# Layer 0's mixture of experts: the output bias row and the running counts of the experts as matrix products, and a shorter gating sum

## The chip, the cores and the metric

The kernel runs on one core of one Trainium2 chip. The metric is the time of one launch on the device, in microseconds (us). Lower is better. A profile of one further execution shows every engine: TensorE (PE, with its weight loads PEld apart), VectorE (DVE), ScalarE (ACT), GpSimd (POOL) and SyncE (SP).

## The reference, cut to what matters

The whole program is a decoder of two layers, each with self-attention, cross-attention and a feed-forward part, over 32 sequences of 100 tokens with 256 features, all in float32. The change lies in the third of these six parts, the feed-forward part of layer 0. That part is itself a small transformer block with a mixture of experts:

```
q, k, v  = in_proj(rope(layernorm(x))) per head     # 16 heads of 16; q, k, v have biases
x1       = layernorm(x + attention(q,k,v) @ out_proj_w.T + out_proj_b)
logits   = x1 @ gate_w.T + gate_b                   # 8 experts
gates    = softmax(logits); keep the two largest, gates unchanged by the others' removal
moe      = sum over the two kept experts of gate * (x1 @ expert_w[e].T + expert_b[e])
result   = layernorm(x1 + moe)
```

The softmax goes over all eight experts, and the two largest of its values weigh the two experts' outputs. Each row of x1 is processed by only two experts, so the kernel writes every row twice into a list that is sorted by expert, and multiplies whole tiles of 128 rows by one expert's weights.

## The kernel before

**The stage.** The 32 sequences lie in 8 groups `g` of 4 (`G = 4`, `T = 100` tokens each). `heads_attention` (line 286) runs the attention as a software pipeline over steps `s` = 0 to 32, one sequence each. Its order of instructions is written out by hand and kept as written on TensorE, VectorE, ScalarE, GpSimd and the DMA queue. A step does, for the sequence `s + 1`, `scores` (32 x 100 products, line 363), `masked` (VectorE adds the causal mask, line 372), `lowered` (VectorE finds the maximum, line 383; GpSimd subtracts it, line 384) and `exponentials` (ScalarE, line 389); for the sequence `s`, `turn_weights` (TensorE turns the weights in four tiles, line 396; ScalarE copies each, tile `eT`, line 401) and `sums` (line 412); for the sequence `s - 1`, `divided` (TensorE turns, line 425; VectorE takes reciprocals `rc` and divides, tile `o`, lines 430 and 432), `turn_sums` (lines 438 and 444) and `output` (`project`, line 230: two matrix products of `oT` with `f0_wo`, then `res`, line 1396, in which VectorE adds the PSUM tile to the residual rows `xl`). TensorE writes `mm` tiles in PSUM, of which there are four; a product can't start before the tile that it takes is read by its last reader.

**What is filled in.** Between these parts `fill(s, part)` puts other work, by the table `plan`, in which the entry `(i, part)` under the key `away` holds for the group `w + away` with `s = 4 w + i`:

- the norm, rotation and projection of groups that come next (`ahead_norm`, `queries`);
- `output_bias(g)` (line 1401), once for each group, before its first `res` (for group 0 in step 0, for group 1 in step 1, for each later group in the first step of the group before it): VectorE adds the row `out_row` (the output projection's bias and the values' bias times the projection, made once by `output_row`) to the group's 100 x 1024 residual values;
- `rows_of` (the statistics and the norm of finished rows, giving x1) and `gating`, in parts: 0 to 2 turn x1 and form the logits; 5 adds the gate bias, finds the maximum and subtracts it (lines 1450 to 1452); 5.5 takes the exponential (line 1454); 6 sums, inverts, multiplies (lines 1458, 1459 and 1461, tile `gt`) and finds the two largest (`top2`, lines 1109 and 1110); 6.5 makes the one-hot masks `hot`, copies the gates (line 1469) and, on GpSimd, forms `hs` and `hc`, the counts of each expert by row and by sequence; 7 sums these by three products with the triangle and the ones of `before0` (lines 1481, 1485 and 1489); 8 adds the counts of earlier groups `base` (lines 1498 and 1502), picks the place of each row by the one-hot masks (lines 1504 and 1505) and casts it to an integer `pos0` (line 1506);
- `send0`: GpSimd writes the rows of one sequence to their places by two indirect DMAs (line 1517), in steps 12 to 32 in every step, after its last `lowered` of the step;
- `table`, in the last steps: VectorE makes the list of tiles.

**After the attention** the loop over tiles of 128 rows runs (`turned0`, `product`): TensorE turns a tile, multiplies it by one expert's weights, and the result goes back to DRAM. The gating of the last two groups runs between these tiles.

**What sets the order.** All queues are in order. The instruction that waits holds back all that stands behind it on its engine.

Of the kernel before, what the change touches and what calls it, by code (L numbers as in the profile page):

```python
# [10 lines left out]
F32 = mybir.dt.float32  # L11
# [7 lines left out]
P = 128  # L19
B, T, D = 32, 100, 256  # L20
S2, DC = 361, 192
G = 4
# [44 lines left out]
def kernel(ctx: ExitStack, tc: tile.TileContext, io: dict, out: bass.AP):  # L67
# [215 lines left out]
        load_x(g)  # L283


    def heads_attention(pool, w, wo, bias, norm, turn, res, fill, ready=0, order=()):

# [160 lines left out]
        def output(s):  # L448
            oT = oTs.pop(s)
            ps = mm_tile()  # L450
            project(ps[:T, :D], [oT[:, k, :] for k in range(2)], [wo[:, k, :] for k in range(2)])
            res(s, ps[:T, :D])

        fill.queries, fill.turned = queries_or_keys, turned_
# [81 lines left out]
    def list_of(g):  # L536

        return int(g >= SPLIT[1])
# [776 lines left out]
    with tc.tile_pool(name="f0x", bufs=1) as fixed, tc.tile_pool(name="f0", bufs=2) as pool:  # L1315
# [31 lines left out]
                shift[:, c, :], less[:, c : c + 1].to_broadcast([P, P]), 1.0 / D, None, ALU.mult  # L1347
            )

        out_row = fixed.tile([T, D], F32, name="out_row")  # L1350
        nc.sync.dma_start(out_row, io["f0_bo"].to_broadcast([T, D]))

        def output_row():
            own = fixed.tile([P, 2, T], F32, name="own_values")
            for c in range(2):
                nc.vector.tensor_scalar(
                    own[:, c, :], col("f0_bv", c).to_broadcast([P, T]), 1.0, None, ALU.mult
                )
            ps = mm_tile()
            project(  # L1360
                ps[:T, :D], [own[:, c, :] for c in range(2)], [f0_wo[:, c, :] for c in range(2)]
            )
            nc.vector.tensor_tensor(out_row, ps[:T, :D], out_row, ALU.add)

        biases, heldx = {}, {}

# [29 lines left out]
            nc.vector.tensor_tensor(xi, xi, ps, ALU.add)  # L1396

        x1s, x1Ts, parts = {}, {}, {}

        def output_bias(g):  # L1400
            nc.vector.tensor_tensor(xls[g], xls[g], bc(out_row, 1, G), ALU.add)

        def rows_of(g, part):

# [15 lines left out]
        def gating(g, part):  # L1420
            if part == 0:
                heldx[g] = [mm_tile() for _ in range(2)]
                for c in range(2):
                    for i in range(G):
                        nc.tensor.transpose(
                            heldx[g][c][:, i * T : (i + 1) * T],
                            x1s[g][:, i, c * P : (c + 1) * P], ident[:T, :T],
                        )
            elif part == 1:
                x1T = x1Ts[g] = pool.tile([P, 2, GT], F32, tag="x1T", name="x1T", bufs=1)  # L1430
                for c in range(2):
                    nc.scalar.activation(
                        x1T[:, c, :], heldx[g][c][:, :GT], AF.Identity,
                        bias=col("f0_ln1b", c), scale=col("f0_ln1w", c),
                    )
            elif part == 2:
                x1T = x1Ts.pop(g)
                pg = heldx[g] = mm_tile()
                for i in range(G):
                    project(  # L1440
                        pg[:T, i * E : (i + 1) * E],
                        [x1T[:, c, i * T : (i + 1) * T] for c in range(2)],
                        [f0_wg[:, c, :] for c in range(2)],
                    )
            elif part == 5:
                pg = heldx.pop(g)
                lg = parts[g] = small.tile([T, G, E], F32, tag="lg", name="lg")
                p3 = pg[:T, : G * E].rearrange("p (g e) -> p g e", e=E)
                nmx = small.tile([T, G], F32, tag="nmg", name="nmg")
                nc.vector.tensor_tensor(lg, p3, bc(row("f0_gb"), 1, G), ALU.add)  # L1450
                nc.vector.tensor_reduce(nmx, lg, AX.X, ALU.max, negate=True)
                nc.vector.tensor_tensor(lg, lg, bc(nmx, 2, E), ALU.add)
            elif part == 5.5:
                nc.scalar.activation(parts[g], parts[g], AF.Exp)
            elif part == 6:
                lg = parts.pop(g)
                sm = small.tile([T, G], F32, tag="smg", name="smg")
                nc.vector.tensor_reduce(sm, lg, AX.X, ALU.add)
                nc.vector.reciprocal(sm, sm)
                gt = small.tile([T, G, E], F32, tag="gt", name="gt")  # L1460
                nc.vector.tensor_tensor(gt, lg, bc(sm, 2, E), ALU.mult)
                parts[g] = top2(pool, gt, G)
            elif part == 6.5:
                own = slice(g * G, (g + 1) * G)
                top, hot = top2(
                    pool, None, G, row("iota", P), which0[:, :, own].rearrange("t k g -> t g k"),
                    parts[g],
                )
                nc.gpsimd.tensor_copy(gates0[:, own, :], top[:T, :, 0:2])
                hs = pool.tile([T, G, E], F32, tag="hs", name="hs")  # L1470
                hc = pool.tile([T, G + 1, E], F32, tag="hc", name="hc")
                nc.gpsimd.tensor_tensor(hs, hot[:T, 0], hot[:T, 1], ALU.add)
                nc.gpsimd.memset(hc[:, 0], 0.0)
                for i in range(G):
                    nc.gpsimd.tensor_tensor(hc[:, i + 1], hc[:, i], hs[:, i], ALU.add)
                parts[g] = hot, hs, hc
            elif part == 7:
                hot, hs, hc = parts[g]
                pl = heldx[g] = mm_tile()
                n = G * E  # L1480
# [4 lines left out]
                nc.tensor.matmul(  # L1485
                    pl[:, :n], before0[:, 1, :], hc[:, :G].rearrange("p i e -> p (i e)"),
                    start=False, stop=True,
                )
                nc.tensor.matmul(
                    pl[:, n : n + E], before0[:, 1, :], hc[:, G], start=True, stop=True  # L1490
                )
            else:
                hot, hs, hc = parts.pop(g)
                pl = heldx.pop(g)
                n = G * E
                base = base0[list_of(g)]
                at = pool.tile([T, G, E], F32, tag="at", name="at")
                nc.vector.tensor_tensor(
                    at, pl[:T, :n].rearrange("p (i e) -> p i e", e=E), bc(base[:T], 1, G),
                    ALU.add,  # L1500
                )
                nc.vector.tensor_tensor(base, base, pl[:, n : n + E], ALU.add)
                own = slice(g * G, (g + 1) * G)
# [151 lines left out]
        def ahead_norm(g, part):  # L1655
# [10 lines left out]
                (3, 3): ((ahead_norm, 3.1),),  # L1666
            },
            1: {
                (0, 2): ((ahead_norm, 3.2), (output_bias,)), (1, 1): ((queries, 0),),
                (1, 2): ((queries, 1),), (2, 1): ((queries, 2),), (2, 2): ((queries, 3),),  # L1670
            },
            0: {(3, 2): ((rows_of, 0),)},
# [15 lines left out]
        def fill(s, part):  # L1688

            w, i = s // G, s % G  # L1690
            if s == 0 and part == 0:
                output_row()
            for away, events in plan.items():
                g = w + away
                if 0 <= g < NG and (away < 1 or g >= 2):
                    for f, *args in events.get((i, part), ()):
                        if s < B or f is not gating:
                            f(g, *(args if s < B or f is not send0 else (1,)))
            if s < 2 and part == 2:
                output_bias(s)  # L1700
            if s == B and part == 0:
                send0(SPLIT[1], 0)
            if (s, part) in CONSTANTS:
                make_constants(CONSTANTS[s, part])
            if s < 2 * E and s % 2 == 0 and part in (1, 2):
                expert_weights(s // 2, part - 1)
                if part == 2 and s // 2 + 2 < E:
                    expert_bias(s // 2 + 2)
            first = G * (SPLIT[1] + 2)
            if part == 2 and 0 <= s - first < 5:  # L1710
                table(0, s - first)
            if (s, part) in ((B - 1, 3), (B, 1)):
                for n in range(AHEAD // 2):
                    fetch((s - B + 1) * (AHEAD // 2) + n)
# [1194 lines left out]
```

## Time and profile before

| what | us |
|---|---|
| median of 3 runs | 3312.29 |
| lowest and highest run | 3305.76 and 3319.2 |
| the profiled execution's own time | 3304.47 |
| its span, first to last instruction | 3302.7 |
| `scores` of the 2nd step to `scores` of the last one, in the profile | 758.13 to 1024.06 |

The span is cut into lines of code: a row of the profile names the line, the engine, the operation, the tile that is written and the tiles that are read, the shape, the number of instructions, their busy time and the mean of one, and then the idle time of the engine just before them, with what ended it. A row "A <- B" among the waits says that A's engine stood idle until B was done. The granted clock is TensorE's, 1.00 at full speed; its mean over the span is 0.982.

### The profile page before, as it was taken

The numbers are of one execution on the slowest core, as the hardware profiler recorded it, in microseconds if no ns is written. First come the engines' busy times: TensorE is split into PE (matmuls) and PEld (weight loads), VectorE is DVE, ScalarE is ACT, GpSimd is POOL, SyncE is SP. The second block draws the span as 40 slices with busy tenths as digits, with TensorE's granted clock in tenths as the row PEclk, the third lists the DMA queues.
The fourth block names the chain that finished last, engine by engine and source line by source line (L and its number), as shares of the span: only waits on it lengthen the run. The fifth ranks groups of instructions, "written<-read, shape, count | busy, mean of one in ns | idle before, by whom it ended". The sixth has DMA issues, their size and how long they took to land. (4 is left out here: it accounts for less than half of the span.)

```text
span 3302.7 us, 66245 instructions
## 1 busy us (share of the span) xinstructions
PE 3155.7 (96%) x25158; PEld 2155.8 (65%) x25158; DVE 1823.4 (55%) x5227; ACT 1660.2 (50%) x3701; POOL 1335.6 (40%) x1191
## 2 busy tenths in 40 slices
PE   8998999989998899998999999999999999999998
PEld 6775666656776543334666666666666667899998
DVE  6777666758886578875446555564656451011111
ACT  5665666666664366674555554454555442211111
POOL 3445888866775532201223333333333332012222
PEclk9999999999998999998999999999999999999999
DMA  9401211101012722001000100000000003456665
GB/s 301 158 15 55 56 51 51 48 21 40 25 35 74 220 70 53 26 1 46 10 15 22 34 15 25 17 28 24 16 26 21 25 13 107 134 183 189 179 181 159
DMA packets 165700, 228.71 MB, mean 69 GB/s; under 512 B 22846, under 2 KB 139618, under 8 KB 164998
## 3 DMA queue, kind: packets, MB, share of 16 engines
q1 hardware_dynamic: 133592, 185.22, 18.0%
q0 software_dynamic: 20304, 27.99, 4.0%
q10 hardware_dynamic: 11486, 11.23, 1.0%
q8 instruction: 204, 3.34, 0.4%
q14 instruction: 114, 0.93, 0.1%
HBM read 150.92 MB, written 73.41 MB: 68 GB/s over the span
## 5 line engine op out<-in xcount | busy, mean ns | idle before, releaser
L2289 POOL TENSOR_TENSOR ex<-ex,rc 100x1444 f32<-100x1444 f32 x128 | 331.6, 2591 | 769.5 <-DVE rc L2288 532.0
L2280 ACT ACTIVATE ex<-s,nmx 100x361 f32<-100x361 f32 x512 | 303.2, 594 | 121.6 <-DVE nmx L2271 121.6
L384 POOL TENSOR_TENSOR s<-s,nmx 100x800 f32<-100x800 f32 x128 | 199.6, 1561 | 206.2 <-DVE nmx L383 110.9
L1852 ACT ACTIVATE h<-sc,cols 128x800 f32<-128x800 f32 x256 | 222.0, 924 | 93.1 <-PE sc L1846 91.4
L2740 POOL DMA_INDIRECT out_x<-y,xg x53 | 83.0, 1565 | 425.3 <-DVE y L2739 243.8
L2271 DVE CUSTOM_DVE_ANT_0 s<-sc,mb 100x361 f32<-100x361 f32 x512 | 250.7, 528 | 7.5 <-PE sc L2264 7.5
L2722 ACT ACTIVATE hgT<-sc 128x1024 f32<-128x1024 f32 x53 | 54.3, 1024 | 326.1 <-PE sc L230 326.1
L2739 DVE TENSOR_SCALAR y<-mm,gx 128x256 f32<-128x256 f32 x53 | 25.7, 484 | 323.2 <-PE mm L230 323.2
L230 PE MATMUL sc<-xgT,w1b 128*128 128x128 f32 x1696 | 198.1, 275 | 0.5 <-DMA w1b<-in_f_w 0.5
L2264 PE MATMUL sc<-kT,qT 64*100 64x361 f32 x1024 | 197.6, 463 | 0.0
L230 PEld LDWEIGHTS sc<-xgT,w1b 128*128 128x128 f32 x1696 | 193.6, 192 | 0.8 <-DVE xgT L2707 0.7
L230 PE MATMUL mm<-wx,hgT 128*128 x848 | 191.6, 379 | 0.0
L2236 PE MATMUL mm<-x_wa,cT 128*128 128x512 f32 (+1 forms) x512 | 188.8, 491 | 0.2
L2314 PEld LDWEIGHTS mm<-eT,vb 128*64 128x64 f32 (+1 forms) x3072 | 136.8, 137 | 67.3 <-issue 66.4
L2206 PE MATMUL mm<-cT,x_wa 128*128 128x361 f32 x512 | 179.7, 470 | 1.0 <-ACT lnT L142 0.9
L2296 PE MATMUL mm<-ident,ex 100*128 100x100 f32 (+1 forms) x1536 | 166.6, 257 | 10.1 <-ACT kT L2218 5.5
L2303 ACT COPY eT<-mm 128x400 f32<-128x400 f32 (+1 forms) x256 | 125.6, 491 | 100.1 <-PE mm L2296 98.5
L230 PEld LDWEIGHTS mm<-wx,hgT 128*128 128x128 f32 x848 | 157.2, 190 | 19.2
L2314 PE MATMUL mm<-eT,vb 128*64 128x100 f32 (+1 forms) x3072 | 162.3, 254 | 0.0
L2296 PEld LDWEIGHTS mm<-ident,ex 100*128 100x128 f32 (+1 forms) x1536 | 143.3, 152 | 28.7 <-ACT kT L2218 7.4
L181 POOL TENSOR_TENSOR rs<-va,neghalf 100x4 f32<-100x4 f32 (+1 forms) x95 | 92.7, 978 | 168.2 <-DVE va L177 71.0
L2252 DVE COPY vb<-mm 128x512 f32<-128x512 f32 x64 | 44.2, 691 | 193.2 <-PE mm L2241 193.2
(427 smaller groups left out, 7244.3 us busy)
## 6 DMA issues: line engine op xcount, KB each, us to landing
w1b<-in_f_w SPq DMA_DIRECT2D x55, 1024.0 KB
rows_dram<-zero SPq DMA_DIRECT2D x32, 896.0 KB
cT<-in_ctxT SPq DMA_DIRECT2D x64, 180.5 KB
cT<-in_ctxT SPq DMA_DIRECT2D x128, 90.2 KB
xg<-rows_dram SPq DMA_DIRECT2D x65, 128.0 KB
y_dram<-y ACTq DMA_DIRECT2D x65, 128.0 KB
wx<-in_f_w SPq DMA_DIRECT2D x8, 1024.0 KB
xg<-sorted_dram SPq DMA_DIRECT2D x57, 132.5 KB
```

The lines of the kernel that those rows point to most:

```text
L230: nc.tensor.matmul(ps, lhsT[k], rhs[k], start=(k == 0), stop=(k == n - 1))
L384: nc.gpsimd.tensor_tensor(sm, sm, bc(nmx, 2, T), ALU.add)
L1852: nc.scalar.activation(h1, both[r2][:, :, :GT], AF.Tanh, bias=col("a1_b1", o))
L2206: nc.tensor.matmul(kTs[u][c][:, :S2], x1_wa[:, m * P : (m + 1) * P], cT[:, 0, :], start=True, stop=False,)
L2236: nc.tensor.matmul(ps[e][:kn, :n], cT[:, 0, at], x1_wa[:, 1024 + c0 : 1024 + c0 + n], start=True, stop=False,)
L2264: nc.tensor.matmul(ps[:T, e, :S2], qT[p0 : p0 + 64, m, tok], kT[p0 : p0 + 64, c, :], start=True, stop=True,)
L2271: nc.vector.tensor_tensor_reduce(s[:, e, :], ps[:T, e, :S2], mb, 1.0, 3.4e38, ALU.add, ALU.min, nmx[:, e : e + 1],)
L2280: nc.scalar.activation(ex[:, 2 * c + e, :], s[:, e, :], AF.Exp, bias=nmx[:, e : e + 1], scale=-1.0, accum_out=sm[:, 2 * c + e : 2 * c + e ...
L2289: nc.gpsimd.tensor_tensor(ex, ex, bc(rc, 2, S2), ALU.mult)
L2296: nc.tensor.transpose(pt[:kn, j * T : (j + 1) * T], ex[:, j, k0 : k0 + kn], ident[:T, :T])
L2303: nc.scalar.copy(dst, pt[:kn, :GT])
L2314: nc.tensor.matmul(po[64 * e : 64 * e + 64, m * T : (m + 1) * T], vb[k][:kn, v0 + 64 * h : v0 + 64 * h + 64] if k < 2 else vb[2 + u % 2][: ...
```

## The change

- `output` takes one more product: the rows of the tile `alike`, all 1/128, times `out_row`, which now fills all 128 partitions. The sum over the 128 partitions is the bias row, and it is added to the output's PSUM tile. `output_bias` and its eight VectorE instructions are removed.
- Part 5 no longer subtracts the maximum. ScalarE takes it as the bias of the exponential, in one instruction for each of the group's four sequences, and gives the sum as well (`accum_out`).
- Part 6 no longer sums and multiplies: `top2` looks at the exponentials as they are, and GpSimd multiplies the two found gates by the inverse sum, in place of the copy.
- Part 7 takes one more product, `alike` times the running counts `base`. Part 8 multiplies the masks by the PSUM tile at once, in two instructions. GpSimd, not VectorE, casts the places to integers.

```diff
         def output(s):
             oT = oTs.pop(s)
             ps = mm_tile()
-            project(ps[:T, :D], [oT[:, k, :] for k in range(2)], [wo[:, k, :] for k in range(2)])
+            project(
+                ps[:T, :D], [oT[:, k, :] for k in range(2)] + [a for a, _ in more_out],
+                [wo[:, k, :] for k in range(2)] + [b for _, b in more_out],
+            )
             res(s, ps[:T, :D])
...
-        out_row = fixed.tile([T, D], F32, name="out_row")
-        nc.sync.dma_start(out_row, io["f0_bo"].to_broadcast([T, D]))
+        out_row = fixed.tile([P, D], F32, name="out_row")
+        nc.sync.dma_start(out_row, io["f0_bo"].to_broadcast([P, D]))
+        alike = fixed.tile([P, P], F32, name="alike")
+        nc.gpsimd.memset(alike, 1.0 / P)
...
-        def output_bias(g):
-            nc.vector.tensor_tensor(xls[g], xls[g], bc(out_row, 1, G), ALU.add)
...
                 nc.vector.tensor_tensor(lg, p3, bc(row("f0_gb"), 1, G), ALU.add)
                 nc.vector.tensor_reduce(nmx, lg, AX.X, ALU.max, negate=True)
-                nc.vector.tensor_tensor(lg, lg, bc(nmx, 2, E), ALU.add)
+                parts[g] = lg, nmx
             elif part == 5.5:
-                nc.scalar.activation(parts[g], parts[g], AF.Exp)
+                lg, nmx = parts[g]
+                sm = small.tile([T, G], F32, tag="smg", name="smg")
+                for i in range(G):
+                    nc.scalar.activation(
+                        lg[:, i, :], lg[:, i, :], AF.Exp, bias=nmx[:, i : i + 1],
+                        accum_out=sm[:, i : i + 1],
+                    )
+                parts[g] = lg, sm
             elif part == 6:
-                lg = parts.pop(g)
-                sm = small.tile([T, G], F32, tag="smg", name="smg")
-                nc.vector.tensor_reduce(sm, lg, AX.X, ALU.add)
+                lg, sm = parts.pop(g)
                 nc.vector.reciprocal(sm, sm)
-                gt = small.tile([T, G, E], F32, tag="gt", name="gt")
-                nc.vector.tensor_tensor(gt, lg, bc(sm, 2, E), ALU.mult)
-                parts[g] = top2(pool, gt, G)
+                parts[g] = *top2(pool, lg, G), sm
...
-                nc.gpsimd.tensor_copy(gates0[:, own, :], top[:T, :, 0:2])
+                nc.gpsimd.tensor_tensor(
+                    gates0[:, own, :], top[:T, :, 0:2], bc(sm, 2, 2), ALU.mult
+                )
...
                 nc.tensor.matmul(
                     pl[:, :n], before0[:, 1, :], hc[:, :G].rearrange("p i e -> p (i e)"),
-                    start=False, stop=True,
+                    start=False, stop=False,
+                )
+                nc.tensor.matmul(
+                    pl[:, :n], alike, bc(base0[list_of(g)], 1, G), start=False, stop=True
                 )
...
-                at = pool.tile([T, G, E], F32, tag="at", name="at")
-                nc.vector.tensor_tensor(
-                    at, pl[:T, :n].rearrange("p (i e) -> p i e", e=E), bc(base[:T], 1, G),
-                    ALU.add,
-                )
+                own = slice(g * G, (g + 1) * G)
+                for k in range(2):
+                    nc.vector.tensor_tensor(
+                        hot[:T, k], pl[:T, :n].rearrange("p (i e) -> p i e", e=E), hot[:T, k],
+                        ALU.mult,
+                    )
+                nc.vector.tensor_reduce(exact0[:, :, own], hot[:T], AX.X, ALU.add)
+                nc.gpsimd.tensor_copy(pos0[:, :, own], exact0[:, :, own])
                 nc.vector.tensor_tensor(base, base, pl[:, n : n + E], ALU.add)
-                own = slice(g * G, (g + 1) * G)
-                nc.vector.tensor_tensor(hot[:T], hot[:T], bc(at, 1, 2), ALU.mult)
-                nc.vector.tensor_reduce(exact0[:, :, own], hot[:T], AX.X, ALU.add)
-                nc.vector.tensor_copy(pos0[:, :, own], exact0[:, :, own])
...
         heads_attention(
             attn, f0_w, f0_wo, ("f0_bq", "f0_bk", "f0_bv"), norm, turn_group, res, fill, 2,
-            (pool_, sp_),
+            (pool_, sp_), ((alike[:, :T], out_row),),
         )
```

More of the change, by code (lines that the diff above doesn't have):

```diff
@@ L283, with heads_attention @@
         load_x(g)
-    def heads_attention(pool, w, wo, bias, norm, turn, res, fill, ready=0, order=()):
+    def heads_attention(pool, w, wo, bias, norm, turn, res, fill, ready=0, order=(), more_out=()):
         qTs, kTs, vas, sms, exs, eTs, backs, oTs, turned_ = {}, {}, {}, {}, {}, {}, {}, {}, {}
@@ L1348 @@
             )
-        out_row = fixed.tile([T, D], F32, name="out_row")
-        nc.sync.dma_start(out_row, io["f0_bo"].to_broadcast([T, D]))
+        out_row = fixed.tile([P, D], F32, name="out_row")
+        nc.sync.dma_start(out_row, io["f0_bo"].to_broadcast([P, D]))
+        alike = fixed.tile([P, P], F32, name="alike")
+        nc.gpsimd.memset(alike, 1.0 / P)
         def output_row():
-            own = fixed.tile([P, 2, T], F32, name="own_values")
+            own = fixed.tile([P, 2, P], F32, name="own_values")
             for c in range(2):
                 nc.vector.tensor_scalar(
-                    own[:, c, :], col("f0_bv", c).to_broadcast([P, T]), 1.0, None, ALU.mult
+                    own[:, c, :], col("f0_bv", c).to_broadcast([P, P]), 1.0, None, ALU.mult
                 )
@@ L1360, in output_row @@
             project(
-                ps[:T, :D], [own[:, c, :] for c in range(2)], [f0_wo[:, c, :] for c in range(2)]
+                ps[:, :D], [own[:, c, :] for c in range(2)], [f0_wo[:, c, :] for c in range(2)]
             )
-            nc.vector.tensor_tensor(out_row, ps[:T, :D], out_row, ALU.add)
+            nc.vector.tensor_tensor(out_row, ps[:, :D], out_row, ALU.add)
         biases, heldx = {}, {}
@@ L1451, in gating @@
                 nc.vector.tensor_reduce(nmx, lg, AX.X, ALU.max, negate=True)
-                nc.vector.tensor_tensor(lg, lg, bc(nmx, 2, E), ALU.add)
+                parts[g] = lg, nmx
             elif part == 5.5:
-                nc.scalar.activation(parts[g], parts[g], AF.Exp)
+                lg, nmx = parts[g]
[6 more added lines that the diff above has]
+                parts[g] = lg, sm
             elif part == 6:
-                lg = parts.pop(g)
-                sm = small.tile([T, G], F32, tag="smg", name="smg")
-                nc.vector.tensor_reduce(sm, lg, AX.X, ALU.add)
+                lg, sm = parts.pop(g)
                 nc.vector.reciprocal(sm, sm)
-                gt = small.tile([T, G, E], F32, tag="gt", name="gt")
-                nc.vector.tensor_tensor(gt, lg, bc(sm, 2, E), ALU.mult)
-                parts[g] = top2(pool, gt, G)
+                parts[g] = *top2(pool, lg, G), sm
             elif part == 6.5:
+                *found, sm = parts[g]
                 own = slice(g * G, (g + 1) * G)
@@ L1466, in gating @@
                     pool, None, G, row("iota", P), which0[:, :, own].rearrange("t k g -> t g k"),
-                    parts[g],
+                    found,
                 )
-                nc.gpsimd.tensor_copy(gates0[:, own, :], top[:T, :, 0:2])
+                nc.gpsimd.tensor_tensor(
+                    gates0[:, own, :], top[:T, :, 0:2], bc(sm, 2, 2), ALU.mult
+                )
                 hs = pool.tile([T, G, E], F32, tag="hs", name="hs")
@@ L1668 @@
             1: {
-                (0, 2): ((ahead_norm, 3.2), (output_bias,)), (1, 1): ((queries, 0),),
+                (0, 2): ((ahead_norm, 3.2),), (1, 1): ((queries, 0),),
                 (1, 2): ((queries, 1),), (2, 1): ((queries, 2),), (2, 2): ((queries, 3),),
@@ L1698, in fill @@
                             f(g, *(args if s < B or f is not send0 else (1,)))
-            if s < 2 and part == 2:
-                output_bias(s)
             if s == B and part == 0:
```

## The prediction

> **What bounds the kernel now.** I first read the head of the page, for the busiest engine, then the busy times of single steps, then what TensorE waits for in this stage, then the order of time where the new products go.
>
> ```profile
> PE 3155.7 (96%) x25158; PEld 2155.8 (65%) x25158; DVE 1823.4 (55%) x5227; ACT 1660.2 (50%) x3701; POOL 1335.6 (40%) x1191
> ```
>
> TensorE is busy all over, but only the changed stage counts. Busy times of the whole stage (first line) and of single steps (PE, PEld, DVE, ACT, POOL, then the granted clock):
>
> ```profile
> 758.13:1024.06 265.93, 246.86 (x3087) 188.37 (x3083) 223.42 (x493) 184.29 (x378) 188.24 (x271) 0.98 0.10 27
> 799.48:808.98 9.50, 9.50 (x108) 6.99 (x107) 6.27 (x14) 6.05 (x13) 5.36 (x8) 1.00 0.01 3
> 953.98:962.61 8.63, 8.63 (x103) 6.22 (x102) 7.83 (x24) 6.16 (x14) 5.99 (x10) 1.00 0.07 20
> 979.85:990.07 10.22, 9.05 (x104) 6.26 (x103) 7.89 (x15) 6.43 (x13) 8.30 (x15) 1.00 0.10 26
> 1015.82:1024.06 8.24, 6.16 (x96) 4.71 (x95) 6.18 (x16) 4.18 (x9) 4.23 (x9) 1.00 0.10 27
> ```
>
> In the steps from 799.48 and 953.98 TensorE has no gap at all. The step from 979.85 follows directly on an `output_bias`; TensorE lacks 1.17 there. The last line is a late step at the same place in its group, but with no `output_bias`; it lacks 2.08. So the gap is not the bias addition's alone. TensorE's waits in the stage, all with what ended them:
>
> ```profile
> PE mm L396 <- ACT eT L401: 6.2, 15, 1.6
> PE mm L396 <- DVE o L432: 5.1, 8, 1.0
> PE mm L412 <- ACT qT L317: 2.0, 5, 0.4
> PE mm L396 <- ACT kT L327: 1.9, 1, 1.9
> PE mm L230 <- DVE o L432: 1.8, 4, 0.5
> PE mm L396 <- DVE xl L1396: 1.2, 4, 0.6
> PE mm L230 <- ACT back L417: 0.2, 1, 0.2
> ```
>
> They add up to 18.4 us of 265.93. That is all that a lighter VectorE could give back here, and TensorE gets more work. What a product costs is read where TensorE has no gap:
>
> ```profile
> 968.05 0.39 PE L1485 MATMUL mm<-hc,before 100*128 100x32 f32 x2
> 968.27 0.37 PE L1489 MATMUL mm<-hc,before 100*128 100x8 f32 x2
> ...
> 971.32 1.03 PE L230 MATMUL mm<-f_wo,oT 128*100 128x256 f32 x4
> 972.28 0.96 PE L363 MATMUL sc<-kT,qT 32*100 32x100 f32 x32
> ```
>
> `output` begins at 971.32 and the next `scores` at 972.28: 0.96 for two products, 0.48 each (two records). The counts' products follow each other by 0.22.
>
> **The bias row on TensorE.** The built order shows 32 new products of 128x256, one in every `output`, and `scores` stands right behind: 32 x 0.48 = +15.4. Where TensorE waits anyway, part of it is covered. Such steps are those in which `masked` comes late because GpSimd writes rows: `masked` starts 0.5 to 0.6 after the second indirect write ends (964.43 after 963.81; 1019.00 after 1018.46). `rc` and `o` stand behind `masked` on VectorE, and TensorE's turned tiles wait for `o`. GpSimd's clock there is set in the step before, so `scores` that come 0.48 later lose less to it. I count the seven steps from 876, 886, 924, 962, 998, 1007 and 1015, at 0.43: -3.0 (bounds 0 and -3.4).
>
> **The counts on TensorE.** 8 x 0.22 = +1.8.
>
> **The bias addition taken from VectorE.** Eight instructions, 18.5 us busy, mean 2317 ns. None ended a wait of another engine by itself; they delay `res`, and with it `masked` and `o`. Step by step, TensorE's gaps in the steps that follow them come to about 5.4 in all, apart from waits for `qT` and `kT`. What is late next? In the first groups nothing but ScalarE's first `eT` copy (gaps of 0.29 stay in steps without an addition), so I take -2.0 there. From the step at 865.99 on, GpSimd's row writes come. Beside the addition the first of them takes 1.67 instead of 0.99, and `masked` slips in before the second. Without the addition both go early, and `masked` may wait until after the second, as in the step from 1015.82. Four steps: from -2.3 (all gaps go) to +5.6 (each becomes 2.08, less today's). I take +1.5, as these steps have 0.4 to 0.5 more lead on GpSimd than that late step. Sum -0.5, bounds -5.4 and +5.6.
>
> The Trainium skill, "SBUF — State Buffer", section "Who interferes with whom", has a rule on this. The row first: `lowered` (L384) takes 2.13 beside the addition at 903.86 and 942.26, and 1.52 without one. The rule says that a VectorE instruction with two SBUF inputs and a GpSimd instruction that reads SBUF block each other; the addition has two, the new multiplications from PSUM have one. By the rule GpSimd gains 8 x 0.61 = 4.9; as ScalarE's exponentials wait for GpSimd, at most that would come off the sum; by TensorE's waits above nothing does, as none of them is ended by GpSimd.
>
> **The gating on VectorE.** Removed, mean ns of one: subtraction 344, sum 164, `gt` 847, `at` 158, half of the product with the masks (641, against two of some 160 from PSUM), the cast 450: about 2.3 for a group, 18 in all. It lies in the steps that hold parts 5, 6 and 8. The step from 953.98 holds part 6, and TensorE has no gap there: nothing. It counts only at the end, from 1024 on, where TensorE has gaps of 1.4 to 1.8 and VectorE runs from `gt` through the masks and the table to `res` without a pause: -1.5 (bounds 0 and -2.5). The table's list is made there too, and the first tile waits for that.
>
> **The gating on ScalarE.** A group's one exponential (0.22) becomes four, each with a read of the sum. No row shows so small a one with a sum; the nearest are L1454 (0.22) and the 189 ns read of L2280. 4 x (0.22 + 0.19) - 0.22 = 1.4 a group. Behind it in ScalarE's queue stand the `eT` copies, on which TensorE waits. Cover: ScalarE stands idle for 0.59 before the first copy (917.55) and the copies come 0.48 later; 0.35 is left, before a product that needs them only after 1.5 us of the projection. I take 0; if that cover fails, 8 x 0.35 = +2.8. Between the tiles after the attention the same 1.4 falls twice where ScalarE is under half busy: 0.
>
> **The gating on GpSimd.** Multiplying instead of copying the gates: 189 ns to about 200. The cast waits for `exact0`; behind it stand the next step's `lowered`, whose maximum VectorE makes later anyway, and in the last step the last group's row writes, which waited for the same places before. `alike` is filled once, long before. All 0.
>
> **The sum.** 15.4 - 3.0 + 1.8 - 0.5 - 1.5 = +12.2. Bounds: 17.2 - 3.4 - 5.4 - 2.5 = +6; 17.2 + 5.6 + 2.8 = +26. On the profiled execution's 3304.5: 3316.7. The median of the runs is 7.8 above that execution, and on it the sum gives 3324.5, which I predict.
>
> **The clock.** One more thing moves either way. These two steps do the same work:
>
> ```profile
> 924.21:935.54 11.33, 10.28 (x118) 8.12 (x117) 7.59 (x23) 6.93 (x15) 9.45 (x20) 0.85 0.23 66
> 962.61:972.28 9.67, 8.67 (x118) 7.14 (x117) 7.40 (x21) 7.82 (x17) 6.64 (x17) 1.00 0.23 66
> ```
>
> At 0.85 a step takes 1.66 longer. Three steps of the stage are so, all of the kind with small products and turned tiles. "TensorE: Matmul & The Clock Gate", Part 1, says that the clock halves after an idle window of some 3.4 us, and that the windows run freely. By this rule no step that is 91% busy should be slow, and denser work should keep the clock up: 5 less. The two lines above speak against reading it so, since equally busy steps differ; I leave it at 0 and put 1.7 a step on both sides, three steps: 5.
>
> **Rivals.**
> *Faster.* VectorE and GpSimd, not TensorE, set the pace: if the waits of 18.4 all go, the three slow steps too (5), and of the stage's end, from 1024 on, another 8 of waits, then 17.2 - 18.4 - 5 - 8 = -14: 3298. For it: VectorE's 223.42 of 265.93, and the addition just ahead of `res`. Against it: steps without any gap, and the late step without an addition with the widest gap. It decides once TensorE's gaps per step exceed the 0.48 added. Chance 0.08.
> *Covered.* The new products fall into waits more widely, not in seven steps but in most, and TensorE's end of stage shrinks with VectorE's work: +3, 3315. Against it: 8.63 of 8.63. Chance 0.20.
> *Slower.* In the four steps `masked` falls behind the second row write as at 1015.82 (+5.6), ScalarE's copies come late (+2.8), nothing is covered, and the slow steps stay: 17.2 + 8.4 + 2 = +28: 3340. Chance 0.30.
> That the change doesn't do what it says is excluded by the built order: 40 more products, 8 additions fewer, 32 exponentials in place of 8.
>
> **How the numbers follow.** The forecast has 0.42. What a measurement of this kernel can tell from no change is about 0.5%, 16.6 us: below 3295.7 is faster, above 3328.9 slower. Of the forecast some 0.27 lies above, since the bounds and the runs' own spread (3306 to 3319) widen it; of the slower rival nearly all: 0.42 x 0.27 + 0.30 x 0.95 = 0.40. Faster: half of the first rival and a little of the spread, 0.05. The rest, 0.55, is no difference. For 8 in 10 the range leaves out the faster rival and the far end of the slower one: 3308 to 3343.
>
> **What would show it.** Right: the step from 953.98 grows from 8.63 to about 9.1 with TensorE still full; `output` to `scores` takes 1.44; VectorE's busy time in the stage falls by some 30 while TensorE's grows by 17. Wrong: if steps without gaps don't grow, the new products are cheaper than 0.48; if the steps after the old additions (865.99, 905.36, 943.76, 979.85) lose their gaps or get gaps over 2, the term of -0.5 is wrong; a stage shorter than 265.9 at the same clock makes the first rival right.

## The result and the profile after

The changed kernel takes 3322.78 us (median of 8 runs, 3316.03 to 3330.58) against 3310.33 of the kernel before in its 8 runs: the ratio is 1.0038, with a 95% interval of 1.0025 to 1.0051, which on 3310.33 is 8 to 17 us more. The forecast was +12.2; measured is +12.5. It lies under the 0.5% that was taken as the least that can be told from no change, but the interval leaves out 1. The profiled execution has a span of 3314.5 us against 3302.7.

The head of the page after, then the busy times by stretch (the stage, then the steps that stand for those shown of before; columns as there):

```profile
PE 3168.1 (96%) x25238; PEld 2166.1 (65%) x25238; DVE 1788.8 (54%) x5187; ACT 1667.7 (50%) x3757; POOL 1333.7 (40%) x1200
```

```profile
797.11:807.04 9.93, 9.93 (x110) 7.32 (x109) 6.27 (x14) 6.04 (x14) 5.79 (x8) 1.00 0.01 2
945.67:957.10 11.43, 9.19 (x105) 6.59 (x105) 5.63 (x12) 7.71 (x16) 7.70 (x15) 1.00 0.10 28
957.10:966.17 9.07, 9.07 (x106) 6.56 (x105) 6.93 (x26) 7.18 (x22) 5.80 (x10) 1.00 0.05 13
1023.76:1032.10 8.34, 6.60 (x98) 5.04 (x97) 6.22 (x16) 4.21 (x9) 4.45 (x5) 1.00 0.09 25
755.99:1032.10 276.11, 258.23 (x3155) 198.93 (x3151) 194.53 (x466) 188.92 (x413) 184.30 (x275) 0.98 0.09 26
```

The step that took 8.63 takes 9.07, the one of 9.50 takes 9.93, and TensorE still has no gap in either: the bias row's product, at its whole length. The late step at 1015.82 of before, which lacked 2.08, grew by 0.10 only. The stage grew by 10.2, and the step ahead of it by another 2.35 (1.7 of that is a stretch of half clock, which the step of before has not). VectorE has 28.9 less to do in it. TensorE's waits in the stage after:

```profile
PE mm L396 <- ACT eT L401: 10.1, 14, 1.8
PE mm L396 <- DVE o L432: 3.8, 7, 0.6
PE mm L412 <- ACT qT L317: 2.0, 5, 0.4
PE mm L230 <- DVE o L432: 1.0, 3, 0.4
```

Waits for `eT` rose from 6.2 to 10.1, those for `o` fell. The line 945.67:957.10 shows where: a step that followed an addition before lacks 2.24 of TensorE now; at 943.76 of before it lacked 1.05 (9.17 of 10.22). The order of time in this step:

```profile
945.90 0.87 ACT L389 ACTIVATE ex<-s 100x800 f32<-100x800 f32 x1 [0.36 <-POOL s L384]
946.19 1.05 POOL L1527 DMA_INDIRECT rows_dram<-x,pos  x1 [0.20 <-POOL pace L1523]
947.05 0.85 PE L396 MATMUL mm<-ident,ex 100*100 100x100 f32 x8
947.54 0.99 POOL L1527 DMA_INDIRECT rows_dram<-x,pos  x1 [0.21 <-issue]
948.37 0.99 DVE L372 TENSOR_TENSOR s<-sc,causal 100x800 f32<-100x800 f32 x1 [3.50 <-PE mm L396]
949.19 0.89 ACT L401 COPY eT<-mm 100x400 f32<-100x400 f32 x2 [1.43 <-PE mm L396]
949.74 0.89 PE L396 MATMUL mm<-ident,ex 100*100 100x100 f32 x8 [1.83 <-ACT eT L401]
```

The two row writes follow each other from 946.19 to 948.53. The `scores` ended at 946.63, but `masked` begins at 948.37, and the first `eT` copy at 949.19, although the tile that it copies was turned by 947.56 and ScalarE was free from 947.76; TensorE waits 1.83. Both rows name TensorE as what ended their wait (`<-PE mm L396`). The trace also has the time of each signal (semaphore update) by which an engine tells the others that a product is done: the one for these `scores` came at 948.28, 1.65 after their end, and those for the two turned tiles at 949.11 and 949.17. So VectorE and ScalarE stood idle for word from TensorE that came late. In the same step of the kernel before:

```profile
942.93 2.54 DVE L1401 TENSOR_TENSOR xl<-xl,out_row 100x1024 f32<-100x1024 f32 x1
944.71 1.67 POOL L1517 DMA_INDIRECT rows_dram<-x,pos  x1 [0.20 <-issue]
945.73 0.98 DVE L372 TENSOR_TENSOR s<-sc,causal 100x800 f32<-100x800 f32 x1
946.69 0.99 POOL L1517 DMA_INDIRECT rows_dram<-x,pos  x1 [0.21 <-issue]
```

Beside the long addition the first write was slow, and `masked` had begun before the second one.

### The profile page after: what moved, and what is told of

The parts are those of the page before. It is cut to its first block, busy times and chain, and to the rows that moved or that the text cites. A ratio compares the mean times of both kernels' runs of the same rounds, so it can differ in the third digit from the quotient of the medians.

```text
span 3314.5 us, 66437 instructions
## 1 busy us (share of the span) xinstructions
PE 3168.1 (96%) x25238; PEld 2166.1 (65%) x25238; DVE 1788.8 (54%) x5187; ACT 1667.7 (50%) x3757; POOL 1333.7 (40%) x1200
## 5 line engine op out<-in xcount | busy, mean ns | idle before, releaser
L2747 DVE TENSOR_SCALAR y<-mm,gx 128x256 f32<-128x256 f32 x53 | 25.7, 485 | 323.3 <-PE mm L230 323.3
L372 DVE TENSOR_TENSOR s<-sc,causal 100x800 f32<-100x800 f32 x128 | 126.1, 986 | 48.2 <-PE sc L363 32.5
```

What stands on the lines that cost most here:

```text
L372: nc.vector.tensor_tensor(sm.rearrange("p (r j) k -> p r j k", r=2), ps[:T, :, :GT].rearrange("p r (j k) -> p r j k", k=T), bc(bc(causal, ...
```

## The experiments

All are read in two ways: the ratio to the kernel before, measured beside it on the same chip, and the stage in the profile, here from the `scores` at 748.12 in before to those at 1024.06, so one step more than above. In every profile TensorE's granted clock is at one half for stretches of 3.41 us. How many of them fall into the stage differs from profile to profile, so the table also gives the length less 1.7 for each of them (half their length; that is too much where TensorE waits anyway, so the last column is good to a few us only where there are many). "Gaps" is the time in which TensorE had neither a product nor a weight load.

| kernel | length | half-clock stretches | gaps | length less 1.7 each |
|---|---|---|---|---|
| before | 275.9 | 3 | 20.2 | 270.8 |
| after | 288.5 | 4 | 20.3 | 281.6 |
| e1, bias row on TensorE only | 290.0 | 4 | 22.9 | 283.2 |
| e2, gating only | 281.3 | 5 | 21.6 | 272.7 |
| e3, after without the bias row | 279.4 | 2 | 25.7 | 276.0 |
| e4, after, bias row in bfloat16 | 288.7 | 5 | 27.1 | 280.2 |
| e5, after, row writes moved | 281.0 | 1 | 17.7 | 279.3 |
| e6, before, row writes moved | 283.6 | 5 | 26.0 | 275.1 |
| e7, after, no row writes | 274.9 | 1 | 12.4 | 273.2 |
| e8, before, no row writes | 266.9 | 1 | 15.6 | 265.2 |
| e9, before without the additions | 282.1 | 7 | 21.1 | 270.1 |
| e10, e9 without row writes | 264.6 | 1 | 14.7 | 262.9 |
| e11, before, additions cut in four | 279.4 | 4 | 23.0 | 272.6 |
| e12, part of the gating and e11 | 279.5 | 2 | 25.4 | 276.1 |

**e1: the bias row alone.** The change without its parts 5 to 8 of `gating`.

> Only the bias row's products and the removal of the eight additions; the gating is that of before. Theory (the products' own length on TensorE sets the price): steps without a gap in the trace of after grew by 0.43 to 0.44, 32 x 0.44 = 14, less some 3 that waits cover, 0 for VectorE: +11, 3321; the steps without a gap grow by 0.43 here too. Rival (the gating carries a good part of the +12.5): +6 or less, 3316.

Ratio 1.0050 (1.0033 to 1.0066), or +16.5 on 3306.5; the stage +12.4, with two gaps of 1.9 that after has not (see e4). Steps without a gap grew by 0.43 here too. So the bias row carries all of the change's price, or more; the rival is out.

**e2: the gating alone.** The kernel before with parts 5 to 8 as changed.

> Only the gating's part, with its eight counts products; the additions stay on VectorE, no bias products. Theory: +1.8 for the counts products, -1.5 at the end of the stage: 0, within 2 of before, 3310; the steps of the stage keep their lengths but for those that hold a counts product, +0.2 each. Rival (ScalarE's four exponentials delay the eT copies, or the casts on GpSimd the row writes): +4 or more, with longer waits of TensorE for eT.

Ratio 1.0015 (0.9998 to 1.0032); the stage +1.9. The time alone can't tell 0 from 4, and the +1.9 is a sum of unlike parts: the first steps are 1.0 shorter, and gaps of 0.69 and 2.23 appear at 896.98 and 972.66. ScalarE's four exponentials do cost something here: the steps at 915.37, 954.02 and 993.45, whose like in before have no gap, grew by 0.3 each, as the first `eT` copy stands behind the exponentials.

```profile
956.32 1.66 ACT L401 COPY eT<-mm 100x400 f32<-100x400 f32 x4
956.85 0.55 PE L396 MATMUL mm<-ident,ex 100*100 100x100 f32 x4 [0.26 <-ACT eT L401]
```

The copy starts 2.30 after the `scores` at 954.02; in before it is 1.97 (955.95 after 953.98). In the changed kernel it is 1.98 again (959.08 after 957.10), because the new product in `output` puts the next `scores` 0.43 later and ScalarE has done part of its work by then. So the exponentials cost nothing only where the bias row's product stands beside them.

**e3: what the 32 products cost.** The changed kernel with the row left out:

```diff
-            (pool_, sp_), ((alike[:, :T], out_row),),
+            (pool_, sp_), (),
```

> The changed kernel with the bias row's 32 products left out (the bias is then missing from the output): what the rest of the change does. Theory: the products alone cost 14 less cover, so this one comes back to before, 3310 within 3. The steps that followed an addition (865.99, 905.36, 943.76, 979.85 of before) keep the gap of about 2.2 that three of them have after, as the addition is missing here too; if that gap comes from the products instead, those steps are back at 1.1. Rival (VectorE's relief is worth 5 or more and was only hidden by the products): 3303.

The time as a whole can't be used (3328.25, 1.0065): with other logits the rows fall to other experts, and in the last part of the program, from layer 1's first expert tile on, 410 us stand where before has 395. In the stage the 32 products are worth 9.1 (288.5 to 279.4), or 5.6 without the half-clock stretches, not 14 (29 of the 32 lie in it, 12.6 at 0.435): the gaps rose by 5.4 when the products went. Neither forecast of the steps held: those that had lacked 2.2 lack 1.7, 1.7 and 1.0 here, and steps that had none before, such as those at 897.92 and 953.98, now lack 1.25 and 0.96. The latter, like 0.96 at 914.91, is a wait for the `eT` copy behind the four exponentials.

**e4: a shorter product.** The row is split into three bfloat16 parts that add up to it, on 96 partitions, and multiplied by 1/32 in bfloat16.

```diff
-            (pool_, sp_), ((alike[:, :T], out_row),),
+            (pool_, sp_), ((like3[:, :T], row3),),
```

> The changed kernel, but the bias row is split once into three bfloat16 parts that together hold its 24 bits, on 3 x 32 partitions, and its product is one in bfloat16 into the same PSUM tile. Theory (the product's length is the price): the distance from output to the next scores falls from 1.4 to about 1.1, and the time by 32 x 0.33 = 10 to 3312. If any further product costs 0.44 whatever its type, 3322 as after. The Trainium skill, FP8 and Floating Point Precision, says that a product of true FP32 takes four passes: a quarter of 0.44 is 0.11.

Ratio 1.0051 (1.0036 to 1.0066): no gain, so the expected 3312 was wrong. Yet the product did get shorter. The row of e4, its step at 799.10 (9.93 after), and a step further on:

```profile
967.75 0.27 PE L231 MATMUL mm<-row,like 96*100 96x256 bf16 x1
```

```profile
799.10:808.71 9.61, 9.61 (x108) 7.11 (x107) 6.27 (x14) 6.05 (x13) 5.47 (x8) 1.00 0.01 3
977.75:987.53 9.78, 7.62 (x113) 6.45 (x112) 8.84 (x10) 4.78 (x11) 5.97 (x6) 1.00 0.07 20
```

Steps without a gap are shorter by 0.32, so a bfloat16 product costs some 0.11 where the float32 one costs 0.43: a quarter, which agrees with the four passes of true FP32 in the Trainium skill, "FP8 and Floating Point Precision", section "TensorE Precision Notes". From step 12 on, where GpSimd writes rows, the gain turned into gaps: the step from 977.75 is 9.78 long with TensorE busy for 7.62, where the changed kernel's took 8.20 with 7.91 busy. The gaps sum to 27.1 instead of 20.3. The gap of this step is not one of late signals: here VectorE's multiplication of the rotation (`xrT`, 128x800, ahead of `masked` in VectorE's queue) takes 3.00, while GpSimd, behind its row writes, does its own two multiplications of the rotation. It takes 1.34 in the changed kernel, where they overlap by 0.5, and 0.98 in e7, where they don't. It takes 2.9 or more, with a gap of 1.9 or more, in two steps each of e1 and e4 and in one each of e2, e3, e5 and e9. The rival, a price of 0.44 whatever the type, fell too.

**e5 and e6: the row writes elsewhere.** After e3 and e4 the suspicion was that in steps with row writes a loop over GpSimd and VectorE sets the pace. In the steps 12 to 29 the two writes are held until `masked` of the next step has run:

```diff
+            if part == 0 and 13 <= s <= 30:
+                send0((s - 1) // G - 3, (s - 1) % G, fill.sms[s + 1, 0][0:1, 0, 0:1])
```

> The changed kernel, with the two row writes of the steps 12 to 29 held back until masked of the next step's scores has run (the copy to pace reads one element of that tile). New theory (in the steps with row writes masked can be held up while two row writes follow each other, and the loop GpSimd, VectorE, GpSimd of some 8.6 us a step then sets the pace instead of TensorE; the removed additions had parted the two writes): masked starts 1.00 after scores in all these steps, TensorE's gaps in the stage fall from 20.3 to some 12, and the time by 5 to 9. Rival (the row writes only show where the lead is short; TensorE's own work sets the pace): within 3 of the changed kernel, and lowered on GpSimd, now behind the writes, makes new waits for eT.

> The same move of the row writes in the kernel before. New theory: the waits of the steps at 876, 886, 924, 962 and 998 go, 4 to 7 less than before: 3303 to 3306. The difference to the changed kernel with the same move is then nearly the whole price of the products, +13 to +16, as no waits are left for them to fall into. Rival (the products' price stays what it was): that difference is +12 or less.

Ratios 1.0047 (1.0035 to 1.0059) for the changed kernel so moved and 1.0049 (1.0036 to 1.0062) for the one before: no gain in the first, a loss of 15 us in the second. Both numbers expected were missed, and both rivals hold. Of the loss of 15 the stage shows 4.3 without half-clock stretches; where the rest lies is not shown, as no profile of the kernel before was taken beside e6. `masked` did start 1.07 to 1.48 after `scores` in all steps of e5 from 869.18 to 1013.66 but one. But GpSimd's other work stands behind the writes now, and gaps came back where it is late: 1.9 at 899.60, where the multiplications of the rotation collide and VectorE's takes 3.23, and 1.5 at 909.69, with 1.1 of waiting for `eT`. The two writes take 2.3 of a step wherever they stand. And with both so moved, no difference is left in the time between the kernel with 32 products more and the one without them (3302.5 and 3302.9); in the last column of the table it is 4.2.

**e7 and e8: no row writes.** The steps 12 to 29 without `send0`.

> The changed kernel with the row writes of the steps 12 to 29 left out (these rows are then missing from the lists and from the output; only the stage's steps are read). New theory: the gaps of 2.2 at 903, 946 and 986 and those of the last steps to 1015 go; the steps of after that follow a removed addition have at most 0.8, as those before the row writes begin. Rival (the gaps come from the missing additions or from the new products themselves): they stay at 2.

> The kernel before with the row writes of the steps 12 to 29 left out (as above). New theory: with no row writes, the additions cost what VectorE's delay of them costs and the products their whole length: the stage, from the second scores on and at the same number of half-clock stretches, is some 13 to 16 shorter than that of the changed kernel without row writes. Rival (the products are covered by other waits): 9 or less.

The same two steps as at 945.67 and 957.10, of e7 and then of e8:

```profile
946.90:956.78 9.88, 9.18 (x105) 6.58 (x104) 5.63 (x12) 7.61 (x16) 3.42 (x7) 1.00 0.01 2
956.78:965.86 9.08, 9.08 (x106) 6.57 (x105) 6.92 (x26) 7.19 (x22) 5.60 (x13) 1.00 0.00 0
```

```profile
938.75:948.96 10.21, 9.16 (x103) 6.26 (x103) 7.88 (x15) 7.56 (x16) 3.85 (x7) 1.00 0.01 2
948.96:957.59 8.63, 8.63 (x103) 6.22 (x102) 7.82 (x24) 6.16 (x14) 4.49 (x7) 1.00 0.01 2
```

The gap of 2.2 is gone: 11.43 became 9.88. So it came from the row writes, not from the missing addition by itself. In e7 and e8 no signal of TensorE in the stage comes more than 0.05 after its product's end; in after 31 of 383 come more than 0.3 late, by up to 1.81, all in steps with row writes. Without the writes the changed step is even 0.33 shorter than that of before. The same step of e10, with neither addition nor product, tells why:

```profile
937.31:947.20 9.89, 8.76 (x104) 6.26 (x103) 5.94 (x13) 7.49 (x16) 3.87 (x7) 1.00 0.01 2
```

The addition's relief is 0.33 here, and the product costs nothing more, as it falls into the gap of 1.13 that is left. In the stages the difference is 8.0 with one half-clock stretch each: the 13 to 16 expected was wrong, and the rival's "9 or less" right. Row writes cost the kernel before 5.6 of its stage and the changed one 8.4. The late step at 1015.82 says the same from the other side: without row writes it takes 6.26, and 6.68 with the change, so there it grows by a whole product; with row writes it took 8.24 and 8.34.

**e9 and e10: the additions alone.** `output_bias` does nothing; e10 leaves out the row writes too.

> The kernel before with the eight additions of the bias row left out and nothing in their place (the bias is missing from the output, rows go to other experts, so only the stage's steps are read). The prediction's term for this was -0.5 with bounds -5.4 and +5.6. New theory (beside the additions the two row writes of a step are parted, and without them masked waits for both): the stage gets longer, from 270.8 without the cost of half-clock stretches to 272 to 275, with gaps that appear in steps that had none (897.92, 915.57, 953.98, 972.28). Rival (VectorE's relief counts): 265 to 269.

> The same without the additions, and without the row writes of the steps 12 to 29 as well. New theory: here the relief is worth all that the steps lost to the additions, some 0.75 each: 265.2 of the run with the additions and no row writes becomes 259 to 261. Rival: no change, as VectorE had time for the additions.

Without row writes, taking eight additions away is worth 2.3 (265.2 to 262.9), less than the 4 to 6 expected. With row writes it is worth 0.7 by the last column. With seven stretches in e9 that is good to some 3 us, but it speaks against the 272 to 275 of the theory of that moment; of the four steps in which it saw new gaps only those at 897.92 and 972.28 of before got them. The rival's 265 to 269 was missed too.

**e11 and e12: candidates.** e11 cuts the additions of groups 2 to 7 into four of one sequence, one in each step; e12 adds the gating's parts on ScalarE and GpSimd, with no product more on TensorE.

```diff
-                (0, 2): ((ahead_norm, 3.2), (output_bias,)), (1, 1): ((queries, 0),),
+                (0, 2): ((ahead_norm, 3.2), (output_bias, 0)), (1, 1): ((queries, 0),),
```

> The kernel before, with the addition of groups 2 to 7 cut into four of 100x256, one in each step of the group before. If VectorE's long addition is what a step loses by (0.75 each in runs without row writes), 2 to 4 less than before; but if the additions also part the row writes, as the new theory has it, the short ones no longer do so and the time is within 2 of before or 2 to 3 above it.

> The kernel before with those of the change's parts that put nothing on TensorE (ScalarE's four exponentials with their sums, GpSimd's product for the found gates; no bias row products, no counts products), and the addition cut in four. It is the candidate for a kernel that beats both: by the prediction's terms for VectorE's and ScalarE's gating -1.5, so 3 to 5 less than before; by the new theory no difference that can be measured, as the row writes set the stage's pace.

Ratios 1.0001 (0.9988 to 1.0014) and 1.0013 (1.0000 to 1.0025). Neither beats the kernel before, as the theory of the row writes had it for both; the 3 to 5 less by the prediction's terms did not come. In e12 that is not the row writes alone: its stage is 3.5 longer than that of e11, and 2.7 of this lies in the three steps with the exponentials (917.62, 955.17 and 995.73), in which TensorE waits 0.9 to 1.0 for the `eT` copy behind them. There is no new product here to cover them.

## Why the prediction was right, step by step

**What bounds the kernel: right where no rows are written, half right where they are.** The forecast rested on steps without gaps, and they grew as it said. In the steps with row writes less work on TensorE (e3, e4) came back as gaps, moved writes (e5, e6) only moved the waits, and the late step grew by a product only when the writes were gone (e7, e8). So a second limit lies close there: the round over `masked`, `lowered`, the rotation and the row writes, on VectorE and GpSimd. It shows as three kinds of gaps: signals of TensorE that come late beside two row writes, the rotation's multiplications on VectorE and GpSimd in each other's way, and `eT` copies that stand behind the exponentials.

**The bias row, +15.4 less 3.0 covered.** A product costs 0.43 to 0.44, not 0.48: the distance between the two starts held a little more than two products. Thirty-two make 13.9. Of the seven steps named as covered, those from 998, 1007 and 1015 grew by 0.09, 0.04 and 0.10, and the one from 876 shrank by 0.49; those from 886, 924 and 962 grew by 0.3 to 0.4 once the half-clock stretches are taken off. That is 0.8 for all seven, so 2.2 was covered. Three steps that had not been named (782, 817 and 935) covered another 1.1. Cover was sized well (3.3 for 3.0), the product was the term set too high, by a tenth: 10.6 instead of 12.4.

**The counts, +1.8.** e2's +1.9 has other causes, and only five of the eight products lie in the stage of the table. Without row writes the steps with such a product grew by 0.60 instead of 0.43, so 0.17 each, 1.4 for eight.

**The additions, -0.5.** e9 gives -0.7. By the steps of after the sum is about 0, of parts that differ more. The steps of the first groups (758, 789, 826) are 2.3 shorter than the product alone would make them, where 2.0 was said. Of the four later ones, three got gaps of 2.2 and grew by 0.75 beyond the product (the one at 905 once its half-clock stretch is taken off), the first by nothing: +2.3 where +1.5 was taken; it is the slower rival's mechanism at under half of its price. The prediction had said that gaps over 2 in these steps make the term wrong, and three have them; that the sum still comes near -0.5 is in part luck. Its bounds were not well founded either: four times 2.08 less today's gaps of 0.70, 1.04, 1.05 and 1.17 is +4.4, not +5.6, and the 5.4 "apart from waits for `qT` and `kT`" is reached only with the 1.9 for `kT`. Measured by itself, in e9, the relief in the three first steps is 1.6. Not foreseen was the step from 748.12, whose gaps rose from 1.70 to 2.86. There the row's values, now on 128 columns, are made beside `lowered`:

```profile
744.85 2.47 POOL L384 TENSOR_TENSOR s<-s,nmx 100x800 f32<-100x800 f32 x1 [0.39 <-DVE nmx L383]
745.59 0.35 DVE L1361 TENSOR_SCALAR own_values<-cols 128x128 f32<-128x128 f32 x2
749.43 0.55 PE L396 MATMUL mm<-ident,ex 100*100 100x100 f32 x4 [2.26 <-ACT qT L317]
```

`lowered` takes 2.47, not 1.52; ScalarE's exponentials, its `qT` and TensorE's turned tiles are late by it. In before, where the row is made on 100 columns, `lowered` keeps its 1.52 and VectorE's two instructions take 0.97 instead of 0.35.

The prediction cited "SBUF — State Buffer" for such a stretch of GpSimd beside VectorE and put its worth between 0 and 4.9. Its row was misread: the `lowered` of 2.13 at 903.86 and 942.26 had begun beside another VectorE instruction with two inputs in SBUF, the sum of the rotation (L801 of before), and it takes 2.13 in the changed kernel too, where no addition follows:

```profile
943.51 0.98 DVE L804 TENSOR_TENSOR xrT<-xrT,xwT 128x800 f32<-128x800 f32 x1
943.74 2.13 POOL L384 TENSOR_TENSOR s<-s,nmx 100x800 f32<-100x800 f32 x1 [0.46 <-DVE nmx L383]
```

So the rule agrees with the trace, but GpSimd did not gain the 8 x 0.61; only the first addition had stretched a `lowered` by itself (2.37 at 758.85).

**The gating on VectorE, -1.5 at the end of the stage.** Not shown either way. VectorE is busy for 17.31 after the last `scores` instead of 19.68, but from there to the first expert tile it is 29.66 before, 28.74 after and 26.4 in e2. Less half of the half-clock time in it these are 22.6, 23.8 and 22.9; that takes off too much, as TensorE waits for a third of this stretch, and three of the new products lie in it.

**The rest.** ScalarE at 0 held in the changed kernel but for a wait of 0.27 at 916.37. The prediction's reason, 0.59 of idle time and 0.48 of the product as cover, fits: in e2, without the product, the copies were late by 0.33 (its 0.35), and each of three steps lost 0.3. For GpSimd at 0 nothing speaks against it. "VectorE falls by some 30" did (28.9), "TensorE grows by 17" did not: by 11.4. Its products there make 12 to 13, and turned tiles count as shorter where they wait less in between (the eight at 949.74 take 0.89, those at 946.71 of before 1.23).

**The sum.** For the stage the working gave 15.4 - 3.0 + 1.8 - 0.5 = +13.7; of its products 29 of 32 and five of eight lie in the stage as the table has it, which leaves 13.9 - 3.0 + 1.1 - 0.5 = +11.5. The profiles show +10.8 without the half-clock stretches, +12.5 with the one that after has more. Outside, the profiles differ by 4.5 less before the first `scores` and 6.2 more in the 1.74 ms from layer 0's last expert tile to layer 1's first, with 10 more of half clock there; e11, which alters nothing in that part, is 4.6 longer there too. So +12.5 against +12.2 is closer than the working deserves: the products were a tenth too dear, VectorE's gain at the end of the stage is not shown, and the later steps lost more than was taken. What the runs confirm is the sign, the price of the products and how little VectorE's relief is worth.

Open stays why the signals are late beside two row writes. The trace shows that `masked` and the `eT` copy waited for TensorE's signals, up to 1.8 after the products' ends (which the profile models), and e7 that the writes are the cause. It does not show what holds the signals back. Row writes further apart, with other work of GpSimd between them, were not tried.

## What to carry to other kernels

Work moved from a half-idle engine to a full one costs its whole length in every step where the full engine has no gap; count those steps first, then those whose wait has another cause. An engine with 84% busy time can still give almost nothing back: look which wait ends last, not how long its instruction is. Where two loops run at nearly the same length, here TensorE's work and the round over GpSimd's row writes, an estimate made instruction by instruction holds only as long as the step stays on one of them: e4 took 0.32 off steps of the first kind and nothing off the time. And a part that is free only beside another one, as the four exponentials beside the new product, is not free alone: e2, e3 and e12 paid for it.

## What the runs showed of the hardware

- While two indirect row writes of GpSimd follow each other (2.3 us), the signals by which TensorE tells that a product is done can come up to 1.8 late in after, against a median of 0.014; VectorE's `masked` and ScalarE's copy from PSUM then start 1.4 to 1.7 late with no work of theirs ahead. With the writes gone no signal is late by more than 0.05 (e7, e8).
- VectorE's 128x800 multiplication of the rotation, with both inputs in SBUF, takes 0.98 alone and 2.9 to 3.2 beside GpSimd's two of 128x400 (e1 to e5, e9).
- A 256-column product in bfloat16, accumulated into a PSUM tile that float32 products had begun, takes about 0.11 of TensorE's time against 0.43 in float32.
- Half-clock stretches are 3.41 us long. Between one and seven of them lay in the same stage of closely related kernels, which makes up to 10 us between two profiles; with one profile of each kernel it is not shown that the edits cause this.
